# Expert places by products alone, less VectorE work in the first layer's front, and gathers and vector work spread over the second layer's attention

## The chip, the cores and the metric

The kernel runs on one core of one Trainium2 chip. The metric is the device time of one execution in microseconds (us). The kernel before took 1167.64 us, the median of three runs (1167.55 to 1169.25).

The core's engines each work through their own queue in order: TensorE (PE: matrix products and transposes), VectorE (DVE), ScalarE (ACT), GpSimd (POOL) and SyncE (SP, which only issues DMAs). Engines wait for each other through semaphores.

## The reference

Two layers on `x` of 4 batches, 512 tokens and 256 columns. A layer modulates a layer norm by vectors made from `c`, adds a gated attention, and then a gated feed-forward part:

```python
h = _layernorm(x) * (1 + ca) + sa
x = x + ga * attention(h)
h = _layernorm(x) * (1 + cb) + sb
x = x + gb * ffn(h)
```

Layer 0 has a linear attention (one vector per batch) and a mixture of 32 experts, of which each token takes 6:

```python
qn, kn = q / norm(q, axis=1), k / norm(k, axis=1)
out = qn * sum(kn * v, axis=1)
# experts
logits = x @ gate_w.T                         # 8 groups of 4; the best 3 groups are kept
probs = softmax(where(group_keep, grouped, 0.0))
topk_w, topk_idx = top_k(probs, 6)
pos = cumsum(one_hot(flat_e)) - 1             # the pair's place within its expert
valid = pos < 48                              # what comes later is dropped
yb = (silu(g) * u) @ w_down                   # g, u = xb @ w_gate_up, for each expert's 48 rows
out = einsum(topk_w * 16, yb[slot]) + (silu(gs) * us) @ ws_down
```

Layer 1 has a causal softmax attention (16 heads of 128) on the same 512 tokens of each batch, and a feed-forward part `silu(x @ gate) * (x @ up) @ down` of 1024 inner columns, whose three weights are cubic splines of control points.

## The kernel before

**Front (layer 0 up to the experts).** A batch's 512 tokens are 4 tiles of 128 rows (`NTT`). For each batch the program issues the norm and its transposed form (`ln_stats`, `normalized`, `ln_transposed`, lines 187 to 232), the linear attention in two halves (483 to 520), the residual (`add_transposed`, 237), the second norm (`moe_input`), the choice of experts (`choose`, 542) and the pairs' places (`place`, 615). `ln_transposed` transposes the normed rows on PE and evicts two blocks of 128x512 from PSUM: the first on ACT (L228), the second on DVE (L232). `choose` copies the logits from PSUM to SBUF (L555) and works on the copy with small DVE instructions; L592 to L595 keep the scores of possible experts and push the others to -100. The selection `selb` (bf16, 0 or 1) is summed over the tiles by a running prefix `pre` and `carry` (L608, L610). `place` makes the places with two products, one with a strict triangle over a tile's rows (L619) and one with ones over the prefix (L622); DVE then subtracts 200 where a pair is chosen (L626), adds 200 and caps at 255 (L628), so that an unchosen place is far out. One-hot comparisons (L650) and products (L654) turn places into lists of tokens, `ixs`. The shared expert's two products (L704) of all batches fill PE between these; they end on ACT (silu) and DVE (L713).

In the front no order is written out: a scheduler places each instruction on its engine's queue by its own costs and priorities, which follow the order of the program. `tc.issue_after(x)` keeps what stands under it behind `x` in its engine's queue or in time of the plan.

**Experts.** 16 pairs of experts, PE's order written by hand (from 944): for each pair gate and up (L805), a transpose (L819) and down (L828), which ACT scales into an output tile `ysb` (L842). A tile of the first 12 pairs is stored twice: by SP to `ytab` (L873) and by an indirect DMA of POOL to `planes` (L858), rows by token, for batch 0. These 12 share two buffers; the last four have one each. `planes` is read back (L912) and summed into `x` of batch 0 (`gated`, L928 to L932), from which layer 1 starts (`norm(0)`).

**Attention of layer 1.** PE's order is written out, head by head (64 steps, the loop from 1510): scores (L1299) of head n, with mask, maximum, exponential and division on DVE and ACT (L1309 to L1316); transposes of the weights (L1331, copied by ACT at L1333), the weighted sum (L1340), the projection of the next head's q and k (`products`) and the output product. The projections and the output product use a seven-product form for 2x2 blocks. It needs sums of weight blocks (`weight_forms`, 1167: L1174, L1176 early in a step, L1180, L1182 late) and of tokens (`token_forms`, L1043), and POOL makes them; `w_q` of a later head is first scaled by ACT (`scale_q`, L761), when its load has landed. The forms have one buffer each.

Beside this the steps carry other work:

- For batches 1 to 3 the routed output is added from `ytab`: 72 indirect gathers of 128 rows each (`gather`, L281), which accumulate into `ysum`. A gather group is one of the 6 choices for the batch's four tiles. Groups stand at the end of steps 1 to 6 (batch 1), 12, 13, 18 to 21 (batch 2), 28, 29, 34 to 37 (batch 3), each waiting for the last eviction of its step's projection (`evicted[n]`).
- At steps 10, 26 and 42 `combine` (290) adds a batch's `ysum` to `x`, and at the next step `norm` makes its statistics and transposes.
- On every second step from 6 on `spline` (1124) builds a block of feed-forward weights: six DVE instructions, then transposes. `ffn_forms` of finished blocks follow at once for three of the units.
- At step 59 the program calls the feed-forward norm of batch 0, `ffn_norm(0)`, without a place behind which it must stand.

**Feed-forward part of layer 1**: 32 blocks in an order written out; the change doesn't touch it.

Of the kernel before, what the change touches and what calls it, by code (L numbers as in the profile page):

```python
# [10 lines left out]
F32 = mybir.dt.float32  # L11
BF16 = mybir.dt.bfloat16
# [68 lines left out]
def kernel(ctx: ExitStack, tc: tile.TileContext, a: dict, out: bass.AP):  # L81
# [99 lines left out]
    last_pow = [None]  # L181
# [4 lines left out]
    def ln_stats(b, name, after):  # L186

        st = small.tile([P, NTT, 6], F32, tag="st", name=f"st_{name}{b}")
        ag = small.tile([P, NTT, 2], F32, tag="ag", name=f"ag_{name}{b}")
        with after_or_not(after):  # L190
            for i in range(NTT):
                nc.vector.bn_stats(st[:, i, :], xs[b][:, i, :])
                nc.vector.bn_aggr(ag[:, i, :], st[:, i, :])
        rs = small.tile([P, NTT], F32, tag="rs", name=f"rs_{name}{b}")
        nc.vector.tensor_scalar_add(rs, ag[:, :, 1], EPS)
        last_pow[0] = nc.gpsimd.tensor_tensor(rs, rs, nhalf, ALU.pow)
        return ag, rs
# [19 lines left out]
    def ln_transposed(pool, psum, tag, layer, b, shift, scale, hT, name, bufs=None, after=None, scalar_after=None):  # L217

        xn = normalized(pool, b, name, bufs, after, scalar_after)
        for k in range(2):  # L220
# [6 lines left out]
            if k == 0:  # L227
                nc.scalar.activation(  # L228
# [49 lines left out]
    def gather(b, r, after):  # L278

        for i in range(NTT):  # L280
            ga = nc.gpsimd.indirect_dma_start(  # L281
                out=ysum[b][:, i, :],
                out_offset=None,
                in_=ytab[:, :],
                in_offset=bass.IndirectOffsetOnAxis(ap=code[:, b * NTT + i, r : r + 1], axis=0),
                compute_op=ALU.add,
            )
            wait_for(ga, [after])

    def combine(b, after):  # L290

        for i in range(NTT):
            y, xi = ysum[b][:, i, :], xs[b][:, i, :]
            with tc.issue_after(after.ins):
                nc.vector.tensor_tensor(y, y, gbr[:, b, :], ALU.mult)
                nc.vector.tensor_tensor(xi, xi, y, ALU.add)
# [5 lines left out]
    with ExitStack() as l0:  # L302
# [22 lines left out]
        carry = fc.tile([P, E], BF16, tag="carry", name="carry")  # L325
        nc.gpsimd.memset(carry, 0.0)
# [65 lines left out]
        def constants():  # L392
# [4 lines left out]
                out=tri, in_=tri, compare_op=ALU.is_gt, fill=0.0, base=0,  # L397
                pattern=[[1, P]], channel_multiplier=-1,
# [78 lines left out]
        def attention_input(b, sp, ps):  # L477
            hT = hTa[b] = sp.tile([P, 2, T], F32, tag="hTa", name=f"hT_a0{b}")
            _, last[b] = ln_transposed(sp, ps, "tr", 0, b, SA, CA, hT, "a0", 3, last[b - 1])
# [44 lines left out]
        def moe_input(b, sp, ps):  # L524

            hTs[b] = new_hT(hp, b, "m0")
            xn, _ = ln_transposed(sp, ps, "tr", 0, b, SB, CB, hTs[b], "m0", 3)
# [14 lines left out]
        def choose(b, ps):  # L542
# [11 lines left out]
            lg = rp.tile([P, NTT, E], F32, tag="lg", name=f"lg{b}")  # L554
            nc.vector.tensor_copy(lg, lgv)  # L555
# [36 lines left out]
            nc.vector.tensor_single_scalar(sel, wt, TINY, ALU.is_ge)  # L592
            nc.vector.tensor_tensor(sc, sc, sel, ALU.mult)
            nc.vector.tensor_scalar(sel, sel, -1.0, 100.0, ALU.add, ALU.mult)
            nc.vector.tensor_tensor(dp[:, :, 0:E], sc, sel, ALU.add)  # L595
# [9 lines left out]
            nc.vector.scalar_tensor_tensor(wt, wt, SCALE, selb, ALU.mult, ALU.mult)  # L605

            pre = rp.tile([P, NTT, E], BF16, tag="pre", name=f"pre{b}")
            nc.vector.tensor_copy(pre[:, 0, :], carry)  # L608
            for i in range(NTT):
                nc.vector.tensor_tensor(  # L610
                    pre[:, i + 1, :] if i + 1 < NTT else carry, pre[:, i, :], selb[:, i, :], ALU.add
                )
            chosen[b] = sel, selb, pre, wr

        def place(b):

            sel, selb, pre, wr = chosen[b]
# [1189 lines left out]
```

## Time and profile before

| | us |
|---|---|
| median of the runs | 1167.64 |
| the profiled execution's own time | 1168.07 |
| its span, first to last instruction | 1166.0 |
| PE busy | 1118.2 (96%) |
| DVE busy | 859.4 (74%) |
| ACT busy | 536.2 (46%) |
| POOL busy | 619.4 (53%) |
| mean granted PE clock | 0.993 |

A line of a group or of the timeline gives line of the program, engine, operation and output<-inputs with their shapes; in brackets, or behind a bar, stands how long the engine had been idle before it and who ended that. A busy PE is not a PE at its peak, since the ends of products are modelled. A float32 product counts as two instructions.

### The profile page before, as it was taken

What the parts mean: (1) busy time and instruction counts of PE and PEld (TensorE: products, weight loads), DVE (VectorE), ACT (ScalarE), POOL (GpSimd) and SP (SyncE); (2) the same over time, 40 slices, a digit from 0 to 9 for tenths busy, and PEclk for the clock granted to TensorE, in tenths of its full rate; (3) what the DMA queues carried; (4) which work ended last, traced back from release to release, by engine and by line L of the source; (5) the groups of instructions that cost most, each with busy time, mean ns of one, the idle gap of its engine ahead of it and who ended that gap; (6) DMA issues with size and microseconds to landing.
All of it is one profiled execution on the core that took longest, in us unless ns stands there. A gap on an engine that the chain in (4) does not pass through costs nothing.

```text
span 1166.0 us, 16905 instructions
## 1 busy us (share of the span) xinstructions
PE 1118.2 (96%) x5220; PEld 821.9 (70%) x5220; DVE 859.4 (74%) x2601; ACT 536.2 (46%) x1373; POOL 619.4 (53%) x944
## 2 busy tenths in 40 slices
PE   6888998989999999999999999999999999999998
PEld 2434354557777787777777777777777777888887
DVE  5688624567878887788877887988877777567765
ACT  3543223335555555554555465555555455333321
POOL 3354124338874857864665975444635655344331
PEclk9998999999999999999999999999999999999999
DMA  8910389734411322420321431012010000000001
GB/s 266 292 61 23 101 238 281 237 106 87 85 47 51 73 69 37 86 73 19 86 37 46 95 64 60 28 37 65 23 46 19 22 16 1 1 1 19 19 1 37
DMA packets 80485, 86.09 MB, mean 74 GB/s; under 512 B 12158, under 2 KB 64748, under 8 KB 80268
## 3 DMA queue, kind: packets, MB, share of 16 engines
q1 hardware_dynamic: 67868, 70.19, 19.2%
q0 software_dynamic: 11712, 13.25, 7.1%
q10 hardware_dynamic: 816, 1.58, 0.4%
q8 instruction: 42, 0.69, 0.3%
q14 instruction: 47, 0.39, 0.1%
HBM read 73.84 MB, written 11.55 MB: 73 GB/s over the span
## 4 chain that ended last, share of the span: by engine, by line
PE 64%; DVE 8%; POOL 3%; ACT 2%; issue 1%; DMA 1%; SPq 0%; ACTq 0%; DVEq 0%; POOLq 0%
PE s L1299 10%; PE o L1340 10%; PE po L1035 7%; PE P0p L1035 6%; PE fP L1035 6%; PE pt L1331 5%; PE P1p L1035 4%; PE P2p L1035 4%; PE acc L1035 3%; PE P0v L1035 3%; PE P2v L1035 2%; PE P1v L1035 2%; DMA w_q<-in_w_q 1%; POOL ysum L281 1%; DVE spw L1130 1%
## 5 line engine op out<-in xcount | busy, mean ns | idle before, releaser
L1314 ACT ACTIVATE p<-s,nm 128x512 f32<-128x512 f32 (+3 forms) x256 | 135.2, 528 | 116.0 <-DVE nm L1311 113.9
L1299 PE MATMUL s<-qk,qk 128*128 128x512 f32 (+3 forms) x512 | 170.1, 434 | 1.4 <-DVE qk L1207 1.3
L1340 PE MATMUL o<-pT,v 128*128 128x512 f32 (+3 forms) x512 | 148.6, 433 | 0.1
L1340 PEld LDWEIGHTS o<-pT,v 128*128 128x128 f32 x512 | 96.8, 190 | 55.0 <-issue 30.6
L1333 ACT COPY pT<-pt 128x512 f32<-128x512 f32 (+1 forms) x192 | 98.3, 512 | 67.8 <-PE pt L1331 66.7
L1311 DVE TENSOR_REDUCE nm<-s 128x1 f32<-128x512 f32 (+3 forms) x256 | 124.0, 485 | 4.0
L281 POOL DMA_INDIRECT ysum<-ytab,code x72 | 113.5, 1576 | 20.4 <-issue 15.2
L1316 DVE TENSOR_SCALAR p<-p,den 128x512 f32<-128x512 f32 (+3 forms) x256 | 116.2, 454 | 3.4
L1331 PEld LDWEIGHTS pt<-ident,p 128*128 128x128 f32 x640 | 81.6, 141 | 34.4 <-issue 10.5
L1331 PE MATMUL pt<-ident,p 128*128 128x128 f32 x640 | 101.7, 273 | 0.4 <-DVE p L1316 0.4
L1309 DVE TENSOR_TENSOR s<-s,mask 128x128 f32<-128x128 f32 x256 | 73.4, 287 | 32.6 <-PE s L1299 32.6
L1174 POOL TENSOR_TENSOR w_p<-w_q,w_k 128x128 f32<-128x128 f32 x63 | 38.6, 613 | 85.2 <-ACT t1p L1213 52.3
L1299 PEld LDWEIGHTS s<-qk,qk 128*128 128x128 f32 x512 | 77.5, 191 | 5.8 <-issue 1.4
L1035 PE MATMUL P0p<-hT_a,w_q 128*128 128x256 f32 x252 | 75.0, 379 | 0.0
L1182 POOL TENSOR_TENSOR w_p<-w_k 128x128 f32<-128x128 f32 x63 | 29.7, 472 | 81.4 <-PE P2p L1035 81.4
L1035 PEld LDWEIGHTS P0p<-hT_a,w_q 128*128 128x128 f32 x252 | 47.5, 190 | 33.1 <-issue 29.9
L1315 DVE RECIPROCAL den<-den 128x1 f32<-128x1 f32 x256 | 40.4, 158 | 38.3 <-ACT p L1314 33.6
L1035 PE MATMUL P1p<-fT,w_p 128*128 128x256 f32 x252 | 64.9, 380 | 2.4 <-POOL w_p L1176 1.3
L1351 ACT ACTIVATE oH<-o,bia 128x512 f32<-128x512 f32 x64 | 43.9, 687 | 42.9 <-PE o L1340 41.7
L1207 DVE SCALAR_TENSOR_TENSOR qk<-P0p,bia,u3p 128x256 f32<-128x256 f32 x63 | 30.4, 482 | 37.4 <-ACT qk L1228 36.4
L1043 POOL TENSOR_TENSOR fI<-it 128x256 f32<-128x256 f32 x30 | 21.8, 726 | 67.1 <-DVE it L1632 67.1
L1035 PEld LDWEIGHTS P1p<-fT,w_p 128*128 128x128 f32 x252 | 47.6, 190 | 9.9 <-issue 1.8
(338 smaller groups left out, 2677.7 us busy)
## 6 DMA issues: line engine op xcount, KB each, us to landing
wg<-in_w_gate_up SPq DMA_DIRECT2D x16, 704.0 KB
w_q<-in_w_q SPq DMA_DIRECT2D x64, 128.0 KB
w_k<-in_w_k SPq DMA_DIRECT2D x64, 128.0 KB
w_v<-in_w_v SPq DMA_DIRECT2D x16, 512.0 KB
wd<-in_w_down SPq DMA_DIRECT2D x16, 352.0 KB
basis<-in_basis SPq DMA_DIRECT2D x8, 640.0 KB
planes<-zero SPq DMA_DIRECT2D x4, 768.0 KB
yr<-planes SPq DMA_DIRECT2D x4, 768.0 KB
```

What stands on the lines that cost most here:

```text
L281: ga = nc.gpsimd.indirect_dma_start(out=ysum[b][:, i, :], out_offset=None, in_=ytab[:, :], in_offset=bass.IndirectOffsetOnAxis(ap=code[:, ...
L1035: nc.tensor.matmul(out, lhsT=lhsT, rhs=rhs, start=start, stop=stop, skip_group_check=shared)
L1299: nc.tensor.matmul(s[:, at[i] : c], lhsT=qk[n, 0][:, i * P : (i + 1) * P], rhs=qk[n, 1][:, : (i + 1) * P], start=True, stop=True,)
L1309: nc.vector.tensor_tensor(s[:, e - P : e], s[:, e - P : e], mask, ALU.add)
L1311: nc.vector.tensor_reduce(nm, s[:, e - w : e], AX.X, ALU.max, negate=True)
L1314: nc.scalar.activation(p, s[:, e - w : e], AF.Exp, bias=nm, accum_out=den)
L1315: nc.vector.reciprocal(den, den)
L1316: nc.vector.tensor_scalar_mul(p, p, den)
L1331: nc.tensor.transpose(pt[:, c : c + P], probs[n, i][:, j * P : (j + 1) * P], ident)
L1333: nc.scalar.copy(pT, pt[:, :w])
L1340: nc.tensor.matmul(o[:, j * P :], lhsT=vs[n // 4][:, j, hc : hc + HD], rhs=pTs[n, j], start=(j == 0), stop=(j == NTT - 1),)
L1351: nc.scalar.activation(oT, o, AF.Identity, bias=bia[:, 2, h : h + 1])
```

## The change

Places: the prefix over tiles goes. `place` now multiplies the selection itself: the triangle over each tile, ones over each earlier tile spread over the later ones, and ones over a carry of earlier batches, which `choose` adds up with DVE for the next batch alone. The triangle's diagonal holds -200, so the product subtracts 200 where a pair is chosen. The logits are read from PSUM without a copy; the kept scores take three instructions for four. In the front's norms (batch 0's first one aside) both transposed blocks are evicted by ACT. The pairs' output tiles `ysb` have four buffers for two.

Attention: gathers are listed singly and issued three or one to a step, one of them after the third part of the projection and up to two after the output product's forms, behind POOL's last weight form and without the wait for DVE. `combine` does two tiles at each of two steps, with their statistics for the norm. The spline is split over two steps, `scale_q` stands behind the last copy of the transposed weights, `ffn_forms` has steps of its own, and `ffn_norm(0)` stands behind step 59's eviction.

```diff
@@ ln_stats, ln_transposed
+        if b in stats:
+            _, ag = stats.pop(b)
+        else:
...
-            if k == 0:
-                nc.scalar.activation(
+            if k == 0 or both:
+                last = nc.scalar.activation(
                     hT[:, k, :], pt, AF.Identity, bias=mv(layer, shift, k, b), scale=mv(layer, scale, k, b)
                 )
@@ gather, combine
-    def gather(b, r, after):
-        for i in range(NTT):
-            ga = nc.gpsimd.indirect_dma_start(
...
-            wait_for(ga, [after])
+    def gather(b, i, r):
+        nc.gpsimd.indirect_dma_start(
...
+    def combine(b, i, after):
+        if i == 0:
+            st = small.tile([P, NTT, 6], F32, tag="st", name=f"st_c{b}")
+            stats[b] = st, small.tile([P, NTT, 2], F32, tag="ag", name=f"ag_c{b}")
+        st, ag = stats[b]
+        y, xi = ysum[b][:, i, :], xs[b][:, i, :]
+        with tc.issue_after(after.ins):
+            nc.vector.tensor_tensor(y, y, gbr[:, b, :], ALU.mult)
+            nc.vector.tensor_tensor(xi, xi, y, ALU.add)
+            nc.vector.bn_stats(st[:, i, :], xi)
+            nc.vector.bn_aggr(ag[:, i, :], st[:, i, :])
@@ constants
+            nc.gpsimd.affine_select(
+                out=tri, in_=tri, compare_op=ALU.not_equal, fill=-200.0, base=0,
+                pattern=[[1, P]], channel_multiplier=-1,
+            )
@@ choose
-            lg = rp.tile([P, NTT, E], F32, tag="lg", name=f"lg{b}")
-            nc.vector.tensor_copy(lg, lgv)
+            lg = lgv
...
-            nc.vector.tensor_single_scalar(sel, wt, TINY, ALU.is_ge)
-            nc.vector.tensor_tensor(sc, sc, sel, ALU.mult)
-            nc.vector.tensor_scalar(sel, sel, -1.0, 100.0, ALU.add, ALU.mult)
-            nc.vector.tensor_tensor(dp[:, :, 0:E], sc, sel, ALU.add)
+            nc.vector.scalar_tensor_tensor(sc, wt, TINY, sc, ALU.is_ge, ALU.mult)
+            nc.vector.tensor_scalar(sel, wt, TINY, -1.0, ALU.is_ge, ALU.add)
+            nc.vector.scalar_tensor_tensor(dp[:, :, 0:E], sel, 100.0, sc, ALU.mult, ALU.add)
...
-            pre = rp.tile([P, NTT, E], BF16, tag="pre", name=f"pre{b}")
-            nc.vector.tensor_copy(pre[:, 0, :], carry)
-            for i in range(NTT):
-                nc.vector.tensor_tensor(
-                    pre[:, i + 1, :] if i + 1 < NTT else carry, pre[:, i, :], selb[:, i, :], ALU.add
+            if b + 1 < B:
+                c = carry[b + 1] = rp.tile([P, 1, E], BF16, tag="carry", name=f"carry{b}")
+                parts = [selb[:, i, :] for i in range(NTT)] + ([carry[b][:, 0, :]] if b else [])
+                nc.vector.tensor_tensor(c[:, 0, :], parts[0], parts[1], ALU.add)
+                for x in parts[2:]:
+                    nc.vector.tensor_tensor(c[:, 0, :], c[:, 0, :], x, ALU.add)
@@ place
-            nc.vector.scalar_tensor_tensor(sel, selb, -200.0, pos, ALU.mult, ALU.add)
-            nc.vector.tensor_scalar(posb, sel, 200.0, 255.0, ALU.add, ALU.min)
+            nc.tensor.matmul(pos, lhsT=tri, rhs=selb, start=True, stop=False)
+            if b:
+                nc.tensor.matmul(
+                    pos, lhsT=ones, rhs=carry[b].to_broadcast([P, NTT, E]), start=False, stop=False
+                )
+            for i in range(1, NTT):
+                nc.tensor.matmul(
+                    pos[:, i:, :],
+                    lhsT=ones,
+                    rhs=selb[:, i - 1 : i, :].to_broadcast([P, NTT - i, E]),
+                    start=False,
+                    stop=(i == NTT - 1),
+                )
+            nc.vector.tensor_scalar(posb, pos, 200.0, 255.0, ALU.add, ALU.min)
@@ down
-                    [P, D], F32, tag=("ysb", "ysd")[direct], name=f"ysb{q}", bufs=(2, NDIR)[direct]
+                    [P, D], F32, tag=("ysb", "ysd")[direct], name=f"ysb{q}", bufs=4
@@ attention
-        gathers = {r + 1: (1, r) for r in range(TOPK)}
-        for b in range(2, B):
-            for r, n in enumerate((-4, -3, 2, 3, 4, 5)):
-                gathers[(b - 1) * NH + n] = (b, r)
+        gathers, combined_at = {}, {}
+        for b in range(1, B):
+            todo, first_step = [(b, i, r) for r in range(TOPK) for i in range(NTT)], (0, 12, 28)[b - 1]
+            for n, m in enumerate((3,) * 8 if b == 1 else (3, 3, 1, 1, 1, 1, 3, 3, 3, 3, 1, 1)):
+                gathers[first_step + n] = [todo.pop(0) for _ in range(m)]
+            for i in range(NTT):
+                combined_at.setdefault(b * NH - 7 + i // 2, []).append((b, i))
+
+        def gather_some(n, m):
+            with tc.issue_after(last_form[0].ins):
+                for _ in range(min(m, len(gathers.get(n, ())))):
+                    gather(*gathers[n].pop(0))
...
             project(n + 1, 2)
+            gather_some(n, 1)
...
-            scale_q(n + 3)
+            with after_or_not(last_copy[0]):
+                scale_q(n + 3)
             with tc.issue_after(last_form[0].ins):
                 out_prepare(n)
+            gather_some(n, 3)
...
+            if n % 2 and 5 <= n and unit < 3 * NCH:
+                with tc.issue_after(evicted[n].ins):
+                    spline(unit, 0)
+            if n in (10, 26, 42):
+                with tc.issue_after(last_form[0].ins):
+                    ffn_forms(n // 16, early[:, n // 16])
             if n % 2 == 0 and 6 <= n and unit < 3 * NCH:
                 with tc.issue_after(evicted[n].ins):
-                    spline(unit)
-                if unit in (1, 4, 7):
-                    ffn_forms(unit // 3, early[:, unit // 3])
+                    spline(unit, 1)
...
-            if n in gathers:
-                gather(*gathers[n], evicted[n])
+            for b, i in combined_at.get(n, ()):
+                combine(b, i, evicted[n])
...
-                if n % NH == 10:
-                    combine(n // NH + 1, evicted[n])
...
             if n == NHD - 5:
-                ffn_norm(0)
+                ffn_norm(0, evicted[n])
```

## The prediction

> **What bounds the kernel now.** I read the page's head first, then the busy time by stretches, then what TensorE waited for in each stretch.
>
> ```profile
> span 1166.0 us, 16905 instructions
> ...
> PE 1118.2 (96%) x5220; PEld 821.9 (70%) x5220; DVE 859.4 (74%) x2601; ACT 536.2 (46%) x1373; POOL 619.4 (53%) x944
> ```
>
> TensorE (PE) is busy for 96% of the span, so what is to be gained lies in its gaps. The stretches (start:end, length, busy time of each engine with its count, granted clock, DMA share, GB/s) show where these are: the first layer's front with attention and routing (40 to 125, what lies before starts up), the rest of its shared products (125 to 150), the experts (150 to 240), the second layer's attention (262 to 985) and its feed-forward part.
>
> ```profile
> 40.00:125.00 85.00, 70.74 (x286) 34.70 (x285) 71.33 (x277) 35.20 (x62) 37.95 (x58) 0.96 0.38 116
> 125.00:150.00 25.00, 25.00 (x85) 9.87 (x84) 12.77 (x41) 3.57 (x6) 7.90 (x8) 1.00 0.20 53
> 150.00:240.00 90.00, 82.81 (x462) 46.84 (x460) 42.95 (x150) 29.73 (x72) 29.36 (x33) 0.98 0.84 260
> ...
> 262.00:985.00 723.00, 716.16 (x3413) 558.69 (x3411) 580.43 (x1732) 386.42 (x1047) 457.52 (x704) 1.00 0.22 51
> ```
>
> PE idles for 14.3 us of the front's 85, where VectorE (DVE) is as busy as PE; not at all from 125 to 150; for 7.2 us of the experts; for 6.8 us of 723 in attention. Who ended these waits (total us, times, longest), first for 40 to 125:
>
> ```profile
> PE pix L654 <- DVE oh L650: 3.0, 5, 0.9
> PE su L704 <- DVE sT L713: 2.7, 2, 1.6
> PE lt_m L226 <- DVE xn_m L212: 2.5, 4, 1.0
> PE lt_a L226 <- DVE xn_a L212: 1.9, 2, 1.5
> PE pos L622 <- DVE pre L610: 1.9, 2, 1.6
> PE sg L704 <- ACT sT L712: 1.1, 2, 0.7
> PE lt_m L226 <- DVE ssum L587: 1.0, 1, 1.0
> ```
>
> Nearly all end on DVE: 14.1 us. For 150 to 240 there is one line; below it one of the waits of ScalarE (ACT) that stand behind it, in order of time (start, length, instruction, idle time before it); then the five lines for 262 to 985:
>
> ```profile
> PE y L828 <- ACT ysb L842: 4.2, 4, 1.9
> ```
>
> ```profile
> 188.87 0.95 ACT L842 ACTIVATE ysb<-y,xg 64x256 f32<-64x256 f32 x2 [3.70 <-DMA ytab<-ysb]
> ```
>
> ```profile
> PE P2v L1035 <- DVE v L1206: 2.0, 2, 1.9
> PE P1p L1035 <- POOL w_p L1176: 1.3, 1, 1.3
> PE P2p L1035 <- POOL oWTrue L1367: 1.2, 2, 0.6
> PE P1p L1035 <- DVE x L248: 1.1, 2, 0.6
> PE s L1299 <- DVE qk L1207: 0.7, 2, 0.5
> ```
>
> Attention's 723 us thus hold 6.3 us of waits: 64 heads of some 11.3 us, each at PE's own pace. The largest gain that the change could have is the sum of these lists, some 25 us.
>
> **The front, on DVE.** By the groups of DVE there: the copy of the logits goes, 4 x 286 ns = 1.1 us. Of four instructions around the kept scores (341, 392, 216 and 409 ns, four times: 5.4 us) three remain (nearest row, a 128x128 of two inputs, 281 ns, twice, and 216 ns: 3.1 us): 2.3 us. The running prefix goes (4 x 168, 12 x 377 and 4 x 284 ns: 6.3 us), eleven adds for the carry come (at 377 ns, 4.1 us): 2.2 us. The subtraction after the product goes, 4 x 281 = 1.1 us. Seven evictions of transposed rows go to ACT: 7 x 806 = 5.6 us off DVE, 7 x 0.77 = 5.4 us onto ACT, which is at 35 of 85 us. In all DVE loses 12.3 us of work.
>
> That is work; what PE gets is less. The wait of the place product on the prefix (1.9 us) goes whole: the products read the selection itself. The one-hot comparison's 3.0 us stays: a comparison of 0.97 us a chunk is longer than its four products. The other five lines, 9.2 us, end on DVE work (or on ACT behind it) that stands in its queue behind the removed pieces; DVE loses a seventh of its 71 us there, and a removed eviction or copy shortens a wait of 1 us by its own length at most. I take half, 4.6 us. Against it stand eleven more place products (a 128x128 bf16 step takes 0.06 to 0.2 us): 1.1 us at 0.1, of which I count the 0.4 of the last rows, where PE is full. Sum **-6.1 us**. Bounds: +1 (the freed time is all slack, the products and ACT's double eviction, 0.77 more before each logit product, are not) and -11.1 (both lists gone).
>
> Two rules were weighed here. The rows show no dearer read of PSUM: the logits' copy out of PSUM takes 286 ns, a same-sized op on SBUF 280. [...] The second: the prefix adds took 0.69, 0.61 and 0.65 us at 71 to 73, while POOL ran its row adds, and 0.16 us at 117, with POOL idle. [...]
>
> Of the moved place: its rank chain and the row adds on POOL keep their number and sit with each other before the power for the next batch; by the order of the instructions one such power (done at 50.0 before) now stands behind eight row adds (8 x 0.75 = 6 us) and is done near 55, still ahead of the transposes of its output at 57. Taken as nothing; in the bounds.
>
> **The experts.** Four output tiles for two. PE's 4.2 us of waits end on ACT, and ACT on a store of two pairs before: that of 180.17 was still not there at 188.8, 8.7 us. With four tiles it has four pairs, some 16 us. What hides it: PE's pairs of 4.1 us. All four waits come before 212.4, ahead of the last scatter (214.7), from which the read back of the planes, the sums on DVE and the norm lead to attention without a PE wait between; so they count whole, if the queues keep up. The DMA share here is 0.84 (0.93 from 180 to 200), and the w_q loads come through the same engines: ACT already waits 0.6 us for one at 210. I take **-3.7 us**, bounds -4.2 and -1.
>
> **Attention.** All 72 gathers stay, 1.58 us each and 0.30 to the next, POOL only. They went in fours (7.5 us) at the end of steps 1 to 6, 12, 13, 18 to 21, 28, 29 and 34 to 37; now they go one and two at a time at steps 0 to 7, 12 to 23 and 28 to 39, ahead of weight forms of the same step, past POOL's queue only; SP's is not passed. POOL's other work is, from its groups, 2.0 (forms of w_q and w_k), 0.7 (of w_v) and 2.5 us (output product) a head on average, 5.4 with the rest. With four gathers that is 12.9 us against a step of 11.35, with three 11.0. The first shows: in order of time the form w_p came 4.4 us before its product after the first gathers and 0.3 at the last; at 501.9 it came too late:
>
> ```profile
> 496.91 1.56 POOL L281 DMA_INDIRECT ysum<-ytab,code  x1 [0.31 <-issue]
> ...
> 497.90 1.06 POOL L1056 TENSOR_TENSOR wF<-uT 128x128 f32<-128x128 f32 x1
> ...
> 501.37 0.45 POOL L1176 TENSOR_TENSOR w_p<-w_k,w_p 128x128 f32<-128x128 f32 x1
> ```
>
> Between the two stood four forms of `ffn_forms` (L1056 to L1059), which now have steps of their own without gathers (10, 26, 42). With three gathers the 1.3 us go, and the 1.2 us at 380 and 570, where four gathers and four token forms (3 us) stood together. The combine (8 x 0.41 us at one step, then 4 x 0.57 of statistics and a norm at the next) becomes 2.8 us at each of two steps before the norm, and the spline's 3 us split over two steps. The second layer's feed-forward norm for batch 0, which the order put at 756 to 770 (four statistics, a 0.9 us wait for POOL, two 0.7 us scalings on DVE), goes to step 59, where DVE is at 14 of 20 us: the 2.0 us before P2v go. If it is late there, the transposes of the same step wait, 2 us at most. The 0.7 us before the scores go with the lighter DVE. The 1.1 us of the residual stay. The scaling of w_q stands behind the last copy of a step: ACT's 15.0 us of waiting for its load go, worth nothing by themselves (ACT is at 53%); its reader, the form on POOL, is due a third of a step later. Sum 1.3 + 1.2 + 2.0 + 0.7 = 5.2, of which I take **-4.2 us** for what moves elsewhere; bounds -5.2 and +3. The feed-forward part keeps its order: nothing.
>
> **Sum.** -6.1 - 3.7 - 4.2 = -14.0 us. The profiled execution took 1168.07 (span 1166.0 and 2.1 around it), so 1154.1; the runs' median lies 0.4 lower: **1153.7 us**.
>
> **Rivals.**
> - The front gives nothing. PE is full from 125 on, and the waits before may be latency (row statistics, a power on POOL of 1.0 us, scaling) more than DVE's queue. For it: three waits end after such a chain. Against it: DVE at 84%. Then -7.9: 1159.7.
> - DMA paces the experts. For it: share 0.93. Against it: weights are loaded eight pairs ahead. The experts' gain is lost and half of the front's: -7.2, or -5.1 with attention at half: 1160.4 to 1162.5.
> - The change doesn't do what it says: gains and new waits cancel, within 0.2% of before (about what a measurement can tell from no change): 1167.6.
> - Slower: POOL's gathers in the middle of the weight forms. Place: 20 dense steps. POOL has some 0.3 us to spare a step and about 9 us of lead at each spell's start; a spell of eight steps uses it up if a gather takes over about 2.0 us in its new place instead of 1.58. At 2.4 us each dense step loses 2.2 us, 43 in all; less two leads of 9 and the 14 gained: +11, 1179. Against it: gathers ran beside a DVE at 80% already.
>
> **How the numbers follow.** Likeliest 0.63 (1147 to 1160), the front nothing 0.14, DMA 0.12, no change 0.04, slower 0.07. Faster 0.89, same 0.04, slower 0.07. The range goes from 1147 (-20: near the bounds' sum) to 1164, past the DMA case; it leaves out some 0.07 below and 0.12 above.
>
> **What would show it.** The front right: no wait of the place products on DVE, the first expert product about 6 us before 154.7. Wrong: the sT, xn_m lines as long, or waits ended by ACT's hT. The experts right: no y wait on ysb; wrong: ACT waiting for w_q near 205 or read back no earlier. Attention right: no P1p wait on POOL, five lines shrunk to the residual's; wrong: w_p waits at steps 7 to 9 or 18 to 21, lt_f waits at step 59. A gather mean above 1.9 us would make the forecast wrong.

## The result and the profile after

Over 20 executions each the kernel before took 1171.03 us (median) and the changed one 1166.25; the ratio is 0.9955, 95% interval 0.9941 to 0.9968. By the ratio the change is 5.3 us faster (3.7 to 6.9), where 14.0 were forecast. The 20 executions of before lie between 1167.55 and 1176.78 and those of the changed kernel between 1161.69 and 1169.18, so the three runs that the forecast started from were at the low end of its base. The profiled execution of the changed kernel, 1167.14 us, lies in the upper half of its own; against that of before (1168.07) it is only 0.9 us shorter. So the page says where time went, and the ratios say how much.

The head of the page after, and its busy time by stretches (columns as before: start:end, length, busy time of PE, PEld, DVE, ACT and POOL with counts, granted clock, DMA share, GB/s):

```profile
span 1165.3 us, 16892 instructions
PE 1118.4 (96%) x5231; PEld 822.0 (71%) x5231; DVE 873.5 (75%) x2573; ACT 537.1 (46%) x1380; POOL 627.1 (54%) x944
```

```profile
40.00:125.00 85.00, 70.22 (x297) 34.10 (x296) 68.20 (x276) 38.26 (x67) 37.74 (x57) 0.98 0.38 120
...
150.00:240.00 90.00, 83.04 (x459) 46.72 (x458) 44.69 (x154) 31.18 (x73) 32.29 (x36) 0.96 0.84 259
262.00:985.00 723.00, 715.08 (x3402) 556.60 (x3400) 601.97 (x1727) 381.84 (x1046) 460.25 (x700) 1.00 0.21 51
```

DVE has lost work, and is busy for 14 us more (873.5 for 859.4): attention alone holds 21.5 us more DVE time (601.97 for 580.43) with five instructions fewer. PE's waits after, for the front, the experts and attention:

```profile
PE lt_m L229 <- DVE xn_m L215: 4.8, 4, 2.6
PE pix L669 <- DVE oh L665: 3.4, 2, 2.0
PE sg L719 <- ACT sT L727: 2.5, 2, 1.8
PE su L719 <- DVE sT L728: 1.6, 1, 1.6
PE lt_a L229 <- DVE xn_a L215: 1.4, 1, 1.4
PE at_a L247 <- DVE sc L581: 0.6, 1, 0.6
PE pos L628 <- DVE selb L612: 0.3, 1, 0.3
```

```profile
PE gu L820 <- DVE xT L813: 3.2, 1, 3.2
```

```profile
PE P2v L1050 <- DVE v L1228: 4.4, 4, 1.4
PE pt L1353 <- ACT pT L1355: 3.2, 6, 0.8
```

In the front the wait on the prefix (1.9) is gone, and the rest has grown to make up for it: 14.6 us in all, 14.1 before. Of the experts' 4.2 us on `ysb` nothing is left, but the gate product waits 3.2 us for a transposed tile. (Left out from 150 to 240: 0.3 us, and a wait of layer 1's first norm, which comes back under e7.) In attention every wait that was to go has gone (POOL's 2.5, the 2.0 at 771, 0.7 at the scores), and two kinds stand there that were not forecast, 7.6 us in place of 6.3.

The starts of four products cut the execution into five stretches; each profile of this case gives them from its records. In us ("again" is the changed kernel on another chip; the last two columns are variants that come below):

| | before | after | after again | two tiles (e6) | e7 |
|---|---|---|---|---|---|
| start to the first expert product | 154.7 | 151.8 | 152.3 | 149.1 | 152.5 |
| experts: from there to the last down product | 69.9 | 68.4 | 67.3 | 70.0 | 63.7 |
| to the first score product | 23.8 | 25.3 | 24.4 | 22.2 | 24.9 |
| first to last score product | 737.8 | 740.0 | 740.0 | 740.1 | 736.0 |
| to the end | 179.8 | 179.8 | 179.9 | 179.9 | 179.9 |

The changed attention repeats to 0.1 us and is 2.2 us slower than in the profile of before. That figure hangs on the one profile: in six variants below whose attention is that of before (e1, e2, e5, e9, e10, e11) the stretch took 738.6 to 741.1. The last stretch does not move. Between the two profiles of the changed kernel everything that differs lies ahead of the scores.

PE's records also say what the stretches consist of. The records of the granted clock have spells of 3.4 or 6.8 us at 0.50, and each of them but the one at the very end stands behind a wait of PE. Two of the changed kernel, first the wait and then the clock behind it (the columns of the second row are those of the stretches; 0.50 is the clock):

```profile
91.63 0.35 PE L669 MATMUL pix<-oh,tok 128*32 128x384 bf16 x4 [1.97 <-DVE oh L665]
92.80:96.00 3.20, 3.20 (x14) 1.74 (x13) 1.79 (x4) 0.00 (x0) 0.00 (x0) 0.50 0.00 0
```

```profile
204.51 1.81 PE L820 MATMUL gu<-wg,xT 128*64 128x352 f32 x8 [3.19 <-DVE xT L813]
205.50:208.70 3.20, 3.20 (x16) 1.54 (x14) 2.27 (x11) 0.91 (x3) 0.93 (x3) 0.50 0.85 126
```

Half of the time that PE works in such a spell is our estimate, from the 0.50, of what the spell costs. Take the waits and this loss from the experts' stretch, and 62.9 to 63.9 us are left in every profile of this case, whatever the kernel. So the stretch differs by these two alone (us, waits and loss): before 4.2 and 1.7, after 3.5 and 1.7, after again 2.5 and 1.5, e6 4.8 and 1.7, e7 0.4 and none.

### The profile page after: what moved, and what is told of

It reads as the page before. It is cut to its first block, busy times and chain, and to the rows that moved or that the text cites. A ratio compares the mean times of both kernels' runs of the same rounds, so it can differ in the third digit from the quotient of the medians.

```text
span 1165.3 us, 16892 instructions
## 1 busy us (share of the span) xinstructions
PE 1118.4 (96%) x5231; PEld 822.0 (71%) x5231; DVE 873.5 (75%) x2573; ACT 537.1 (46%) x1380; POOL 627.1 (54%) x944
## 4 chain that ended last, share of the span: by engine, by line
PE 74%; DVE 11%; ACT 2%; DMA 2%; issue 1%; POOL 1%; SPq 0%; ACTq 0%; DVEq 0%
PE s L1321 10%; PE o L1362 10%; PE po L1050 7%; PE fP L1050 6%; PE P0p L1050 6%; PE pt L1353 6%; PE P2p L1050 4%; PE P1p L1050 4%; PE P0v L1050 3%; PE acc L1050 3%; PE P1v L1050 2%; PE P2v L1050 2%; PE pd L734 2%; PE gu L820 1%; PE y L843 1%; DVE p L1338 1%
## 5 line engine op out<-in xcount | busy, mean ns | idle before, releaser
L1338 DVE TENSOR_SCALAR p<-p,den 128x512 f32<-128x512 f32 (+3 forms) x256 | 124.3, 486 | 2.6
L283 POOL DMA_INDIRECT ysum<-ytab,code x72 | 116.2, 1614 | 11.3 <-issue 6.1
L1353 PEld LDWEIGHTS pt<-ident,p 128*128 128x128 f32 x640 | 81.3, 141 | 39.2 <-issue 10.5
L1195 POOL TENSOR_TENSOR w_p<-w_q,w_k 128x128 f32<-128x128 f32 x63 | 34.1, 541 | 94.5 <-ACT t1p L1235 84.9
```

The lines of the kernel that those rows point to most:

```text
L283: nc.gpsimd.indirect_dma_start(out=ysum[b][:, i, :], out_offset=None, in_=ytab[:, :], in_offset=bass.IndirectOffsetOnAxis(ap=code[:, b * N ...
L1338: nc.vector.tensor_scalar_mul(p, p, den)
L1353: nc.tensor.transpose(pt[:, c : c + P], probs[n, i][:, j * P : (j + 1) * P], ident)
```

## The experiments

Each was timed in five rounds beside the kernel before on the same chip. The medians of before differ between chips (1169.4 to 1173.3), so the ratios are compared, and a gain in us is ratio less one times that median.

**The three parts alone.** e1 is the kernel before with the front's hunks (those for `both`, the triangle, `choose` and `place`), e3 with all hunks from the gathers on, and e2 with this one:

```diff
-                    [P, D], F32, tag=("ysb", "ysd")[direct], name=f"ysb{q}", bufs=(2, NDIR)[direct]
+                    [P, D], F32, tag=("ysb", "ysd")[direct], name=f"ysb{q}", bufs=4
```

> The kernel before with the front's part of the change alone (places by products, three instructions for the kept scores, no logit copy, both evictions on ScalarE). Step 1 of the prediction: 6.1 us faster, the first expert product about 6 us before 154.7. Reading of the changed kernel's trace: only 2.9 us reach the first expert product (151.8), because waits on the place sums went and waits on xn_m (4.3 for 1.9 us) and on ScalarE's sT (2.8 for 1.4) grew; then the time falls by 2 to 3 us. Rival, front all slack: within 1 us of before.

> The kernel before with four ysb tiles for two, nothing else. Prediction: 3.7 us faster, no wait of the down products on ysb. Rival read from the changed kernel's trace (ScalarE waits 4.4 us for a w_q load near 203 with the next silu behind it, and TensorE 3.4 us behind that): a gain of 1 to 1.5 us, the wait moved from ysb to that load.

> The kernel before with the second layer's part alone (gathers in ones to threes, combine and spline in two halves, scaling of w_q behind the last copy, the norm of the feed-forward part behind step 59). Prediction: 4.2 us faster. Theory from the changed kernel's trace: about 2 us slower, because 4.2 us of new waits on ScalarE's pT copies and 2.9 us more on v evictions replace the 5 us that went; the stretch from the first to the last score product takes 740.0 us instead of 737.8.

| | ratio to before | 95% interval | us |
|---|---|---|---|
| e1, front | 0.9935 | 0.9909 to 0.9960 | -7.6 |
| e2, four tiles | 1.0027 | 1.0008 to 1.0046 | +3.2 |
| e3, attention | 0.9992 | 0.9974 to 1.0009 | -0.9 |

By its times the front's part is worth about what was forecast for it (6.1; the interval is 4.7 to 10.7 us). In its profile 3.1 us stand ahead of the first expert product (151.6): 1.7 are a spell at half clock less, 1.4 an earlier start of the first `lt_m` product. Another 3.1 stand between there and the first score, where nothing was changed: again 1.7 for a half-clock spell that before has at 190.1 and e1 has not, and 1.4 of a shorter wait of layer 1's first norm. Its three fastest executions (1162.3 to 1163.0) have a mean granted clock of 0.997, which none of the 23 of before beside it reaches (0.985 to 0.995); at 0.988 to 0.993 it took 1164.5 to 1170.3. How much of the 7.6 us is the front's own work, and how much such spells, these runs don't show. Attention's part is worth nothing that the times could show: its stretch took 739.9 us, as in the changed kernel. The interval (3.0 us faster to 1.1 slower) leaves room neither for the 2 us slower that the trace foretold nor for the 4.2 us of the forecast. The four tiles alone make the kernel slower, which neither theory had.

**The spline in halves.** The changed kernel with the spline whole on every second step, as before:

```diff
-            if n % 2 and 5 <= n and unit < 3 * NCH:
-                with tc.issue_after(evicted[n].ins):
-                    spline(unit, 0)
...
                 with tc.issue_after(evicted[n].ins):
+                    spline(unit, 0)
                     spline(unit, 1)
```

> The changed kernel with the spline whole again at every second step. Theory: the halves' first instructions meet GpSimd's forms and take up to 2.0 us for 0.5, which makes the masks, maxima and pT copies of the same step late; then the six waits of transposes on pT (4.2 us) go and the stretch of scores takes 736 us, the whole 4 us less than the changed kernel. Rival (mere queue order: three more instructions ahead of the masks, whatever their length): the same six waits go, but as many come back at even steps, and the stretch stays within 1 us of 740.

Measured: 0.9906 (0.9878 to 0.9934), -11.0 us; the stretch of scores 736.15. PE's waits in its attention (from 262 to 985):

```profile
PE pt L1353 <- ACT pT L1355: 1.4, 1, 1.4
PE P1p L1050 <- DVE x L251: 1.1, 2, 0.6
PE P2p L1050 <- DVE qk L1229: 0.8, 3, 0.3
PE P2v L1050 <- DVE v L1228: 0.4, 2, 0.3
PE pt L1353 <- DVE p L1338: 0.4, 1, 0.4
```

Against the changed kernel 3.8 us of the stretch are gone: the split had cost what the rest of the part gained, and more. How, the spline's groups between 245 and 985 us say, first of before, then of the changed kernel (count | busy us, mean ns | idle before):

```profile
L1130 DVE SCALAR_TENSOR_TENSOR spw<-basis,win,spw 128x256 f32<-128x256 f32 x72 | 42.6, 591 | 0.7
L1132 DVE SCALAR_TENSOR_TENSOR spw<-basis,win,spw 128x130 f32<-128x130 f32 (+1 forms) x48 | 18.1, 377 | 0.6
L1128 DVE TENSOR_SCALAR spw<-basis,win 128x256 f32<-128x256 f32 x24 | 10.5, 436 | 0.0
```

```profile
L1148 DVE SCALAR_TENSOR_TENSOR spw<-basis,win,spw 128x256 f32<-128x256 f32 x48 | 35.6, 741 | 0.3
L1153 DVE SCALAR_TENSOR_TENSOR spw<-basis,win,spw 128x130 f32<-128x130 f32 (+1 forms) x48 | 22.3, 471 | 0.4
L1146 DVE TENSOR_SCALAR spw<-basis,win 128x256 f32<-128x256 f32 x24 | 13.3, 553 | 0.0
L1151 DVE SCALAR_TENSOR_TENSOR spw<-basis,win,spw 128x256 f32<-128x256 f32 x24 | 12.6, 525 | 0.0
```

The same 144 instructions keep DVE busy for 83.7 us instead of 71.1; whole again (e4), for 70.0. One of the six places, in order of time (start, length), DVE's queue and then POOL's in the changed kernel:

```profile
318.49 1.26 DVE L1146 TENSOR_SCALAR spw<-basis,win 128x256 f32<-128x256 f32 x1
...
319.78 0.48 DVE L1148 SCALAR_TENSOR_TENSOR spw<-basis,win,spw 128x256 f32<-128x256 f32 x1
...
320.81 1.96 DVE L1148 SCALAR_TENSOR_TENSOR spw<-basis,win,spw 128x256 f32<-128x256 f32 x1
322.69 0.28 DVE L1331 TENSOR_TENSOR s<-s,mask 128x128 f32<-128x128 f32 x1
```

```profile
318.27 1.32 POOL L1403 TENSOR_TENSOR oH<-oH 128x256 f32<-128x256 f32 x1
...
320.74 1.06 POOL L1202 TENSOR_TENSOR w_p<-w_q,w_p 128x128 f32<-128x128 f32 x1
321.16 1.31 POOL L1404 TENSOR_TENSOR oF<-oH 128x256 f32<-128x256 f32 x1
321.84 1.22 POOL L1195 TENSOR_TENSOR w_p<-w_q,w_k 128x128 f32<-128x128 f32 x1
```

An instruction that takes 0.48 us at 319.78 takes 1.96 beside three forms of POOL, and two of these, `w_p`, take 1.06 and 1.22 us beside it, where the same forms took 0.45 and 0.44 at 238.5 and 235.5. Behind it stands the mask of the next scores, behind that the maximum, the exponential on ACT, and on ACT behind the exponential the copy of transposed weights for which PE waits 0.5 us at 325.0. The two long instructions were 2.3 us over their short form, four times the wait. Two more of the six waits, the longest (0.8 us each, at 469 and 660), stand behind such an instruction of 2.0 us. The other three (0.4 each, at 349, 540 and 731) do not: there a half and the first two tiles of `combine` share a step ahead of the mask, so that queue order has a part in it too. Why the two engines lengthen each other these traces don't show. The prediction weighed such a lengthening for the prefix sums (0.61 to 0.69 us while POOL worked, 0.16 with POOL idle), and not for the vector work that was moved.

The waits on `v` (4.4 us) came with the split too. At three places the next batch's norm stood ahead of the eviction; the first, on DVE:

```profile
362.93 0.16 DVE L206 SCALAR_TENSOR_TENSOR nmr_a<-ag_c,rs_a 128x4 f32<-128x4 f32 x1 [1.16 <-POOL rs_a L199]
...
363.60 0.81 DVE L215 TENSOR_SCALAR xn_a<-x,ag_c,rs_a 128x256 f32<-128x256 f32 x1
...
364.53 0.40 DVE L215 TENSOR_SCALAR xn_a<-x,ag_c,rs_a 128x256 f32<-128x256 f32 x1
364.85 0.41 DVE L1228 TENSOR_TENSOR v<-P2v,u3v 128x256 f32<-128x256 f32 x1
```

DVE idles 1.16 us for POOL's power and scales two tiles, 2.4 us in all, and PE waits 1.4 of them. In before the same chain, with the same 1.16 us, stood a step later (374.5 to 376.5), where no `v` was due. With the spline whole the scheduler places it behind `v` again, and 4.0 of the 4.4 us go.

Whether it is the place of the halves or the split itself that costs, e13 asked: the halves one step later, the first on even steps and the second on odd ones.

> The changed kernel with the spline still in two halves, the first on the even steps from 6 and the second on the next odd step, one step later than in the change. Theory (it is where GpSimd's forms meet the spline's instructions, not the split, that costs): the spline's 144 instructions take 70 to 76 us together instead of 84, the waits of transposes on pT and of products on v fall below 6 us from 10.7, and the stretch of scores takes 736 to 738 us. Rival (a half ahead of the masks of every step makes them late, wherever it stands): as many waits as in the changed kernel, the stretch at 740.

Measured: 0.9956 (0.9936 to 0.9977), the stretch 742.2, the 144 instructions 84.9 us. Here it is the second half that meets POOL, and one of its instructions took 2.98 us for some 0.34:

```profile
462.78 2.98 DVE L1153 SCALAR_TENSOR_TENSOR spw<-basis,win,spw 128x130 f32<-128x130 f32 x1
465.69 0.80 DVE L1338 TENSOR_SCALAR p<-p,den 128x256 f32<-128x256 f32 x1
```

The forecast of 70 to 76 us for this place fell: both places were bad. Waits followed the long instructions again (transposes waited 3.1 us for this `p`, at two such places), but a place without a meeting was not found. So a harmless split is neither shown to exist nor excluded, and how much of the cost is meeting POOL and how much the order of DVE's queue stays open.

**The rest of attention's part.** e3 with the spline whole, everything else of the kernel as before:

> The kernel before with the second layer's part alone as in e3, but with the spline whole. Theory: the gathers and sums spread out are worth 2 us of the 4.2 forecast, the split spline cost 4: the stretch of scores takes 736 us instead of 738 to 739, the whole 2 us less than before. Rival: nothing of it survives without the rest of the change, the stretch stays over 737.5.

Measured: 0.9950 (0.9931 to 0.9969), -5.9 us; the stretch 736.1. So gathers in ones to threes, sums in two steps and the moved norm are worth 1.7 us in the stretch against the profile of before, and 2.5 to 5.0 against the six others with its attention; the timing gives 3.6 to 8.1.

**The experts.** ACT in the changed kernel and in before, where the layer's first scalings of `w_q` stand among the pairs:

```profile
202.99 0.42 ACT L776 ACTIVATE w_q<-w_q 128x256 f32<-128x256 f32 x1 [4.35 <-DMA w_q<-in_w_q]
203.43 0.32 ACT L828 ACTIVATE act<-gu 128x176 f32<-128x176 f32 x1
```

```profile
207.09 0.95 ACT L842 ACTIVATE ysb<-y,xg 64x256 f32<-64x256 f32 x2
208.06 0.42 ACT L761 ACTIVATE w_q<-w_q 128x256 f32<-128x256 f32 x1
```

ACT's order is nearly the same in both: the scaling stands ahead of the same silu, and only one output has moved past it. SyncE issues the load at 197.2 in before and at 192.4 here, and it takes about 10.5 us (it is there just ahead of 202.99). Before, ACT came to the scaling at 208.06, held up by the tiles, and found the load landed; now it is there at 198.6, waits 4.35 us, and DVE stands behind the silu and PE behind DVE. The stall on `ysb` had been the cover of this load: e6 and e7 test it. e6 takes two tiles back in the changed kernel; e7 is e4 with

```diff
         for n in range(3):
-            scale_q(n)
+            with tc.issue_after(last_y[0].ins):    # the last pair's output on ScalarE
+                scale_q(n)
```

> The changed kernel with two ysb tiles as before. If the prediction's step for the experts holds in the changed kernel, this is 2 to 4 us slower than the changed kernel, with the ysb waits of 5 us back. If loads set the pace of the experts with either number of tiles, it is within 1.5 us of it. From the sum of the parts alone (front -7.6, attention -0.9) it is some 3 us faster.

> The changed kernel with the spline whole and with the scaling of the first three heads' w_q kept behind the last expert pair's output on ScalarE. Theory (ScalarE stands at a w_q load with the silu of the next pair behind it): no wait of the gate products on xT, 1 to 3 us less than the whole spline's 1161.7. Rival (the loads themselves are late and the wait moves to expert weights or tokens): within 1 us of it.

> The changed kernel again, on the chip of its variants, with a second profile. Theory: the stretch from the first to the last score product repeats to 0.3 us (740.0), since nothing there waits for a DMA; the experts (68.4 from the first gate product to the last down product) differ by several us between executions, which is what spreads the times of one kernel over 7 us.

On one chip: two tiles (e6) 0.9962 (0.9945 to 0.9979), the changed kernel again (e8) 0.9946 (0.9927 to 0.9964), late scaling with the spline whole (e7) 0.9890 (0.9873 to 0.9908). The first two can't be told apart, as where loads set the pace with either number of tiles: with two, the wait on `ysb` is back and that on `xT` is gone:

```profile
PE y L843 <- ACT ysb L857: 4.8, 4, 2.1
```

So in the changed kernel four tiles are worth 0.8 us by the medians, 1.9 by the ratios, which these intervals don't tell from zero. With late scaling neither wait is left; PE's list from 150 to 240 us of e7 has nothing of the pairs but a rest (its first line is layer 1's first norm):

```profile
PE lt_a L229 <- DMA basis<-in_basis: 3.4, 1, 3.4
PE gu L820 <- issue: 0.4, 1, 0.4
```

The experts take 63.7 us there, 6.1 less than before: 3.8 are waits, 1.7 the half-clock spell behind them. The times lie within 1157.2 to 1159.6, where e4 ran from 1156.3 to 1167.1. That the load made most of e4's spread fits this, but isn't shown: its one profile has only 0.4 us of the wait on `xT` (experts 64.4), and its two slowest executions have a mean clock of 0.988, its two fastest 0.993 and 0.994. From e4 to e7 1 to 3 us were expected; the medians, of two chips, differ by 3.5, the ratios by 1.9, and their intervals overlap. Late scaling with two tiles was not run. In the second profile of the changed kernel the experts differ by 1.1 us from the first, less than expected, with 2.1 us of the `xT` wait for 3.2.

**Why four tiles alone are slower.** In e2 the experts took 75.3 us: PE's waits had grown from 4.2 to 7.1 us, and the half-clock loss behind them from 1.7 to 5.1. The window loads had moved ahead of expert weights on SP; e5 is e2 with them held where they were. Another difference was ACT's issue of the second layer's modulation weights (1.5 MB), at 150.6 us in e2, 149.5 in e5 and 119.4 in before; e9 is e2 with the two memory pools opened in the other order:

```diff
-        xp = ew.enter_context(tc.tile_pool(name="exp", bufs=2))
         m1p = ew.enter_context(tc.tile_pool(name="mod1", bufs=1))
+        xp = ew.enter_context(tc.tile_pool(name="exp", bufs=2))
```

> The kernel before with four ysb tiles, and the three window loads kept behind the third head's w_k load, where they stood before (with the four tiles alone the scheduler had moved two of them ahead of expert weights on SyncE's queue, where one weight issue then took 4.4 us). Theory (the windows made that run slow): 5 to 6 us below that run, 1 to 3 below the kernel before, waits on ysb at most 1 us. Rival (four tiles let stores and loads pile up on the DMA engines): still no faster than before, and TensorE waits 3 us or more behind ysb or a load.

> The kernel before with four ysb tiles, and the pool of the second layer's modulation inputs opened ahead of the pool of the pairs' tiles, so that the larger pairs' pool no longer pushes it into memory that the front still holds. In the two runs of four tiles so far the modulation loads (1.5 MB) were issued at 149 to 151 instead of 119 to 120; here the order of the instructions is the one of before but for the place of one output scaling and the windows. Theory (those loads among the expert weights cost the 3 to 7 us): issue back at 119 to 120, 1 to 5 us faster than before, experts (first gate product to last down product) 66 to 69 us instead of 69.9. Rival (four tiles themselves crowd the DMA engines): slower than before again, experts over 72 us.

e5: 1.0060 (1.0040 to 1.0080), the windows were not it. ACT waited 8.8 us at a `w_q` load, and PE 7.4 behind it for `xT`, as in the changed kernel. e9: 1.0084 (1.0064 to 1.0105), slower still, and yet the loads are back at 118.5. What is late now are the tokens, the first gather of `xg` in before and in e9:

```profile
139.64 1.25 POOL L786 DMA_INDIRECT xg<-table,idx  x1 [20.56 <-DVE idxf L694]
```

```profile
151.96 1.25 POOL L786 DMA_INDIRECT xg<-table,idx  x1 [33.84 <-PE pd L719]
```

In before it starts when its index is there; in e9 behind the first `pd` product, where, as we read it, the front's memory is given back. The first expert product came at 164.8 for 154.7, and the pairs themselves took 68.7. So whichever pool comes last in memory waits: we read this as two more tiles no longer fitting beside what the front still holds, and pushing the modulation loads (e2, e5) or the tokens (e9) behind it; the runs show what came late, not the addresses. The forecast for e9 (1 to 5 us faster) had taken the first for the only one. In the changed kernel the loads stay early (115.4), which we take to come from its front holding fewer tiles (the logit copy and the prefix are gone). That the late modulation loads are what made e2 and e5 slow is argued from their place among the weights alone. The DMA share from 150 to 180 us, 0.98 in e2 for 0.83, does not carry it, since the changed kernel has 0.96 there. The rival, the scaling that stands at a `w_q` load (6.8 us in e2, 8.8 in e5), was not taken out of either.

**The front's two halves.** e10 is the kernel before with the hunks for `both` alone, e11 with those for `choose`, `place` and the triangle alone; e12 is e7 without `both`.

> The kernel before with both transposed blocks of the front's norms evicted by ScalarE, nothing else. The prediction's half of the indirect gain by work: 5.6 of the 12.3 us off VectorE are these evictions, so 1.5 to 2.5 us faster. Rival read from the front's trace (waits on ScalarE's sT grew by 1.4 us, waits on xn_m by 2.4): within 1 us of before, or slower.

> The kernel before with places by products and the lighter choice (no logit copy, three instructions for the kept scores), evictions as before. By the prediction 1.9 us of the wait on the prefix, a share of 6.7 us of VectorE's work (2.5), less 0.4: 3.5 to 4.5 us faster. Theory from the front's trace (the front's gain comes from here alone): 5 to 7 us faster. Rival: 2 us or less.

> The fastest kernel so far (whole spline, late scaling, 1158.2) with the front's second blocks evicted by VectorE again. If ScalarE's evictions are worth what the prediction gives them once the other front work is gone (5.6 of 12.3 us of VectorE's work, half of it), this is 2 to 3 us slower. If they are worth nothing, as alone in the kernel before (ratio 1.0002), it is within 1 us of 1158.

e10: 1.0002 (0.9989 to 1.0016). e11: 0.9957 (0.9942 to 0.9972), -5.0 us. e12: 0.9877 (0.9858 to 0.9897), -14.4 us, 1158.5 us for e7's 1158.2 on another chip. Evicting on ACT is worth nothing that these times can tell, alone or with the rest; the places and the lighter choice carry the front's gain. In e10 the waits only change their names:

```profile
PE pos L619 <- DVE selb L604: 2.9, 2, 2.6
PE pix L654 <- DVE oh L650: 2.0, 2, 1.2
PE sg L704 <- ACT sT L712: 1.7, 3, 0.7
```

e11's profile (1170.0 us) is the slowest of its six executions, and has no gain ahead of the experts to show; its gain is read from its times alone. e7 and e12 are faster than both kernels of this case.

## Why the prediction was wrong

**The base.** 1153.7 was counted from three runs at 1167.6; 20 executions have 1171.0. Taken from there the forecast would have been 1157. The forecast gain was still 2.6 times the measured one.

**The front, -6.1: the size held in the times, the way did not, so the size was luck.** The wait on the prefix went nearly as forecast (1.9, and 0.3 on the selection in its place), the comparison's stayed (3.0, 3.4). (The 14.1 us that the forecast puts on DVE include the 1.1 that end on ACT.) The eleven adds for the carry, put at 377 ns each (4.1 us), took 3.8 us. The failed term is "half of 9.2": the other five lines didn't shrink (with the new `at_a` line 10.9 us now), and the share given to the evictions by their work (5.6 of 12.3 us) can't be told from zero in e10 and e12. Work off a busy engine was priced as time, though most of it was not what PE stood behind: with the evictions on ACT the waits for ACT's `sT` grew from 1.1 to 2.5, and without them (e12) they are 1.1 again. The last one-hot product came 5.5 us earlier (131.2 for 136.7), but 2.6 us more of shared products were left to run behind it (20.6 us from there to the first expert product, 18.1 before). From the first `lt_m` product to the first expert product PE waits 13.5 us after the change and 13.1 before, and 13.6 in e1. So no profile shows the front's gain as waits saved, and why the times fall by 5 to 8 us stays open; executions that lose less at half clock are a part of it in e1.

**The experts, -3.7: lost to a wait behind the one removed.** The step "so they count whole, if the queues keep up" failed at ACT's queue. The forecast saw ACT's 0.6 us for a `w_q` load at 210 and named "ACT waiting for w_q near 205" as a sign of being wrong, but priced it at nothing in the sum: it asked what hides the stores, and not what the stall on them had hidden. The rival, DMA pacing the experts, was right in the place and not in the kind: no expert weight was late for PE; a scaling that nobody needed before 235 us stood in front of a silu. With that moved the experts gain 6.1 us. That is more than the 4.2 us of waits, because a second term was priced at nothing without a reason: the clock, 0.96 in the front and 0.98 in the experts in the rows that the forecast shows. The spell behind the experts' waits cost, by the estimate above, 1.5 to 1.7 us on top of their length in before, in e6 and in both profiles of the changed kernel.

**Attention, -4.2: right in every wait removed, and wrong in what took their place.** POOL's 2.5, the norm's 2.0 and the scores' went. The step that failed is "the spline's 3 us split over two steps", costed at nothing: it cost 14 us of DVE time, 3.8 us of the stretch of scores, and the place of a norm. The bound of +3 for this part held (+2.2 in the stretch). The rival that looked for trouble in POOL's gathers (over 2.0 us each) was not it: they took 1.61 on average.

**The sum.** With the spline whole and the scalings late the same change gives 12.9 us (e7; 10.8 to 14.9), or 14.4 without the evictions (e12; 12.1 to 16.7): two placements cost 8, the split 5.7 of them by the times of e4. That 14 is met so well is partly luck, for the shares are others. The profile of e7 has 6.1 us less than before in the experts (3.7 forecast), 1.8 less in attention (4.2) and 2.3 less ahead of the first expert product (6.1); 1.0 of it is lost again before the first score. The rest of the 12.9 lies in executions without a profile.

## What to carry to other kernels

When a stall goes, list what stands next in that engine's queue and when its inputs land: an instruction that came late enough for its load may now come too soon (198.6 for 208.06 us here), and hold up what is urgent behind it (4.35 us). Vector work that is moved must be priced where it lands, beside what POOL does there: two of the spline's fused operations went from 0.48 to 1.96 us and from 0.34 to 2.98 here. A wait of about 2 us on PE must be priced with the half-clock spell that may follow it (after 2.0 us on `oh`, 3.4 us of it in one profile and 6.8 in another). Work taken off a busy engine is worth what a removal run shows, not its share of busy time.

## What the runs showed of the hardware

- Some of DVE's instructions took four times as long beside POOL's, and more: the prefix sums 0.69 us for 0.16 in before, the spline's 1.96 for 0.48 at 320.8 in the changed kernel and 2.98 for some 0.34 at 462.8 in e13. POOL's `w_p` forms beside the 1.96 took 1.06 and 1.22 us for 0.45 and 0.44. The same lengths came back in both profiles of the changed kernel (1.96 and 2.04 us).
- Spells at half clock stood behind waits of PE. The 16 profiles have 63 spells at a granted clock of 0.50 ahead of the last 20 us of the execution, mostly of 3.4 or 6.8 us (10.2 in e9, 13.7 in e5). In the 6.8 us ahead of each, PE had been idle for 1.5 us or more in all. Not every such wait was followed by one: 1.9 us before a `P2v` product, at 771.3 us in before, was not; the same wait in e9 (780.7) was. After the same 2.0 us on `oh` the spell was 3.4 us in the first profile of the changed kernel and 6.8 in the second. These two profiles lost 1.7 and 5.1 us in this way between the front's first `lt_m` product and the first expert product, so one profile can't tell a gain of 2 us there. What sets on a spell, and its length, these profiles don't show.
- Two things differ between executions of one kernel, and these runs don't separate what each gives to the spread of the times: the waits behind a load (on `xT` 3.2 us in one profile of the changed kernel, 2.1 in the other) and the half-clock spells (1.7 and 5.1 us ahead of the experts). The executions of before lie within 1166.2 to 1176.8, those of e7 and e12, in which neither tiles nor loads hold ACT, within 1157.2 to 1159.8. A lower mean clock goes with a longer time in most kernels: e10's twelve executions run from 1167.4 us at 0.991 to 1173.8 at 0.987; in e12 it doesn't (1158.35 us at 0.992, 1159.82 at 0.993), and in e7 hardly (1157.2 at 0.995 and at 0.992, 1159.6 at 0.994).
